# Attention and feed-forward on one core: the ones product in the projections' bank, GpSimd's additions and DMAs moved within a period, three pieces of the plan moved

## The chip, the core and the metric

The kernel runs on one NeuronCore of a Trainium2 chip. The core has five engines that run side by side, each through its own list of instructions in order: TensorE (PE in the profile; its weight loads are shown apart as PEld), VectorE (DVE), ScalarE (ACT), GpSimd (POOL) and SyncE (SP, which here only issues DMAs). [...] The metric is the device time of one execution in microseconds (us); lower is better.

## What is computed

A transformer block on `x` of shape (4, 1024, 512): attention with 16 heads of 32, then a feed-forward layer (FFN) with dequantised integer weights, each with a layer norm before and after and a residual sum.

```python
scores = jnp.einsum('bsnh,btnh->bnst', k, q) / math.sqrt(HEAD_SIZE)
scores = jnp.triu(scores) + -10000.0 * jnp.tril(ones, k=-1)
attn = jax.nn.softmax(scores, axis=2)
out = jnp.einsum('bnkq,bknh->bqnh', attn, v)
...
x = x + _layernorm(_L0_attn_ref(_layernorm(x), Wqkv, bqkv, Wo, bo))
x = x + _layernorm(_L0_ffn_ref(_layernorm(x), gate_w, gate_scale, up_w, up_scale, down_w, down_scale))
```

Each column of the attention weights is divided by the sum of its exponentials. That sum is what the ones product, the additions and the DMAs of this case make.

## The kernel before

**Steps and periods.** Attention goes by steps `(b, hb, g)`: batch `b` of 4, block `hb` of four heads (4 of them), half `g` of the 1024 queries (512 each): 32 steps. A step has 4 key tiles `c` of 128 when `g` is 0 and 8 when `g` is 1, since later keys are masked. One key tile of one step is a **period**; there are 192, after a run-in of 12 (`LEAD`). The last four tiles of a step (`c >= 4*g`) lie on the diagonal and narrow: 512, 384, 256 and 128 queries.

**A period.** Its body (line 803 on) is written out by hand and sets every engine's order. It goes through two halves `u` of two heads each. In a half, `weights` (346) has PE make scores into a PSUM tile `st`, ACT takes the exponential into the tile `pT` in SBUF (384), and on diagonal tiles GpSimd masks `pT` (386). `maxima` (259) makes the scores `sc` of a later step, and DVE takes their maximum (286, 290). `add_up` (425) adds the preceding tile's `pT` to the step's running total. One entry of the list `later` is taken. In half 0 PE also does `values` (395): the product `po` of the masked `pT` of the tile **before** with `v`. So a mask made in one period is read by PE in the next.

**The sum of exponentials.** `add_up` acts for the tile before. Whole-width tiles (`c <= 4*g`) are added by two accumulating DMAs that GpSimd issues (438), both in half 0; narrower ones by GpSimd itself (441), one pair of heads in each half. These stand on GpSimd's queue between the masks of the two halves. The last tile of a step is not added. Instead `quotients` (472), in the second period of the next step, multiplies the total and the last tile by ones (`sums`, 414): the ones product `pd`, in a bank of the pool `ps_big`. DVE adds `t2` to it (482), and reciprocals (486, DVE) and quotients `o` (489, GpSimd) follow from `later`. The last two steps (`direct`) sum on PE alone, in the bank of `ps_own`.

**PSUM banks.** `ps_big` has two buffers in turn, for `sc`, half of the `st`, transposes and most else. `ps_st` and `ps_acc` have one each. `ps_own` has one, for the first projection of a half: `projected` (238) gives that one out when `state["first"]` is set, and then takes `ps_big`.

**Sum of v.** For the masked part of the softmax, `later_v` (551) makes `vl`, a running sum of `v`, with one DVE scan over 1024 columns (556). `vl` has one buffer: the scan may write it only after GpSimd has used the old one in `sums` (337) of `shared` (339). It is called by `turn_piece` (692) for the second half of `v`.

**The plan.** Projections, norms, transposes and output projections are pieces in lists with a due time and a test when they are ready. `fill_whole` (775) takes at most one piece of `whole` in half 0 of a period; only if there was none does `fill` take a projection at that place. More projections go at the end of the period (842).

**Towards the FFN.** `store_out` (579) norms and stores an output tile; that of the last tile of a batch directly follows its projection. `ffn_stage` (625) makes the first normed rows of the FFN during the last steps: statistics (`mean_rstd`, 70: two instructions on DVE, two on GpSimd), then in the same stage the normed rows (`normalized`, 85, DVE), and in the next stage their transpose (633) and its split into two parts (635, 636). After attention, `ffn` runs the rest, bound by its matmuls (965, 998).

Of the kernel before, what the change touches and what calls it, by code (L numbers as in the profile page):

```python
# [27 lines left out]
def tile_attn_ffn_sandwich(  # L28
# [70 lines left out]
    with ExitStack() as actx:  # L99
# [221 lines left out]
        def masked_part(step):  # L321

            b, hb, g = step
            mT, vl = state["mT", step], state["vl", b, hb]
            pb = ps_big.tile([P, 512], F32, tag="big", name=f"pb_{b}_{hb}_{g}")
            nc.tensor.matmul(pb, lhsT=sel, rhs=mT, start=True, stop=True)
            t1 = e2.tile([P, 512], F32, tag="t1", name=f"t1_{b}_{hb}_{g}")
            nc.scalar.activation(t1, pb, AF.Exp, bias=masked)
            t2 = e2.tile([P, 512], F32, tag="t2", name=f"t2_{b}_{hb}_{g}")

            def counts():
                if g == G - 1:
                    nc.gpsimd.memset(t1[:, 511:512], 0.0)
                nc.gpsimd.tensor_tensor(t2, behind[:, ts(g, 512)], t1, ALU.mult)

            def sums():
                nc.gpsimd.tensor_tensor(t1, t1, vl[:, 512 * g + 1 : 512 * g + 513], ALU.mult)

            def shared():
                sums()  # L340
                count(("shared", step))

            later[:0] = (counts, shared)
            state["extra", step] = t1, t2
# [77 lines left out]
                    stop=stop,  # L422
                )

        def add_up(step, c, u):

            if c == 0 or c == 4 * step[2] + 3 or step in direct:
                return  # L430
            n = width(step, c)
            pairs = [
                [t[:, k : k + 2] for t in (state["sum", step], state["pT", step, c])]
                for k in range(0, HPB, 2)
            ]
            if c <= 4 * step[2]:
                for total, pT in pairs if u == 0 else []:
                    nc.gpsimd.dma_start(total, pT, accum_op=ALU.add)  # L438
            else:
                total, pT = pairs[u]  # L440
                nc.gpsimd.tensor_tensor(  # L441
                    total[:, :, 512 - n :], total[:, :, 512 - n :], pT[:, :, :n], ALU.add
                )

        def finish(step):
            b, hb, g = step
# [25 lines left out]
        def quotients(step):  # L472
            b, hb, g = step
            o = state["o", b, hb]
            t1, t2 = state.pop(("quotients", step))
            if step in direct:
                pd = state["pd"]
            else:
                pd = ps_big.tile([P, 512], F32, tag="big", name=f"pd_{b}_{hb}_{g}")
                sums(pd, state.pop(("sum", step)), 512, True, False)  # L480
                sums(pd, state["pT", step, 4 * g + 3], P, False, True)
            nc.vector.tensor_tensor(t2, pd, t2, ALU.add)

# [77 lines left out]
        def project_out(b, j, half):  # L561
            if half == 0:
                xo = e2.tile([P, H], F32, tag="xo", name=f"xo_{b}_{j}")
                nc.sync.dma_start(xo, x[b, j * P : (j + 1) * P, :])
                state["y"] = e2.tile([P, H], F32, tag="y", name=f"y_{b}_{j}"), xo
            y, xo = state["y"]
            py = projected(f"py_{b}_{j}_{half}")
            by_columns(
                py, [(state["o", b, c][:, ts(j, P)], wo_sb[:, c, ts(half, 256)]) for c in range(HC)]
            )  # L570
            nc.vector.tensor_tensor(y[:, ts(half, 256)], py, bo_sb[:, ts(half, 256)], ALU.add)  # L571
            if half == 0 and ("quarter", b, j) in state:
                state.pop(("quarter", b, j))()
            if half == 1:
                if ("ymv", b, j - 1) in state:
                    store_out(b, j - 1)
                state["ymv", b, j] = mean_rstd(p4, [y], f"o{b}_{j}"), y, xo

        def store_out(b, j):
            mv, y, xo = state.pop(("ymv", b, j))  # L580
            normalized(y, y, mv, 0)
            nc.gpsimd.tensor_tensor(xo, xo, y, ALU.add)
            nc.sync.dma_start(x2[b, j * P : (j + 1) * P, :], xo)
# [40 lines left out]

        def ffn_stage(i):
            if i < GT:
                row = pre["rows"][:, i, :]
                mv = mean_rstd(p4, [row], f"f{i}")
            if i > 0:
                xn = state.pop(("xn2", i - 1))  # L630
                pt = ps_big.tile([P, HC, P], F32, tag="big", name=f"xt2_{i - 1}")
                for c in range(HC):
                    nc.tensor.transpose(pt[:, c, :], xn[:, ts(c, P)], ident)
                hi, lo = (pre[k][:, :, ts(i - 1, P)] for k in ("hi", "lo"))
                nc.scalar.copy(hi, pt)
                nc.vector.tensor_tensor(lo, pt, hi, ALU.subtract)
            if i < GT:
                xn = e2.tile([P, H], F32, tag="xn", name=f"xn2_{i}")
                normalized(xn, row, mv, 0)
                state["xn2", i] = xn  # L640
            if i < 3:

                k = "gud"[i]
                nc.vector.tensor_scalar_add(pre[k], pre["raw"].pop(0), -ZERO_POINT)
                pre["raw"].append(load_raw(*((0, "d", 0), (1, "u", 1), (1, "g", 0))[i]))
            if i == 3:
                pre["raw"].reverse()
# [13 lines left out]

        FULL = 1.75
        lanes = {k: [] for k in ("qk", "v", "out")}
        whole = {k: [] for k in ("rows", "ln", "turn")}
        emitted = {}

        def put(lane, cost, due, ready, f, *args):
            lane.append((cost, due, ready, f, args))

        def count(what):  # L670
            emitted[what] = emitted.get(what, 0) + 1
# [20 lines left out]
        def turn_piece(b, hb, half):  # L692
            turn_v(b, hb, half)
            if half:
                later_v(b, hb)

        NQ = S // 256
        for b in range(B):
# [30 lines left out]
            for j in range(NJ):  # L729
                for half in range(2):  # L730
# [1 line left out]
                    put(lanes["out"], FULL, min(due, n_periods - 1 if j < 4 else n_periods + 9),  # L732
                        lambda p, t=after - 4 + WAIT if j < 4 else after + 4 + WAIT: p >= t,
                        project_out, b, j, half)
            put(lanes["out"], 0.1, due, lambda p: True, store_out, b, NJ - 1)

        def heads(of, p):
            return sorted(
# [34 lines left out]
                most -= 1  # L773

        def fill_whole(p):
            ahead = sorted(heads(whole, p), key=lambda h: h[1] != "rows")
            if ahead:
                piece(whole[ahead[0][1]])
            return bool(ahead)
# [23 lines left out]
        for p in range(-LEAD, n_periods + 1):  # L803
# [4 lines left out]
            if rest:  # L808
                rest.pop(0)()
            state["last"] = bool(before) and before[0] in direct  # L810
            for u in range(2):
                state["first"] = True
                if now and (unit or u == 0):

                    weights(*now, [u] if unit else range(2))
                if unit and now:
                    maxima(*unit, [1 - u])
                elif unit and u == 0:
                    maxima(*unit, range(2), alone=True)

                if before:
                    add_up(*before, u)
                if later:
                    later.pop(0)()
                if u == 0:
                    if p in ends:
                        quotients(ends[p])
                    if before:
                        values(*before)
                        if before[1] == 4 * before[0][2] + 3:  # L830
                            finish(before[0])

                    if not fill_whole(p) and (
                        not now or now[1] - 4 * now[0][2] > 1 or spare[0] > 1.5 * FULL
                    ):
                        fill(p, 1)
# [9 lines left out]
                    look(n)  # L846
            if p > at[B - 1, HC - 1, 0] - LEAD and not pre and not (lanes["qk"] or lanes["v"]):
                ffn_begin()
                for i in range(GT + 1):
                    put(whole["ln"], 0, n_periods, lambda q, t=p + 3 + i: q >= t, ffn_stage, i)  # L850
                put(whole["ln"], 0, n_periods, lambda q: True, check_weights)
        for k in ("rows", "ln", "turn"):
            assert not whole[k], (k, len(whole[k]))
        while later:
            later.pop(0)()
# [267 lines left out]
```

## Time and profile before

| what | us |
|---|---|
| runs | 1966.08, 1966.87, 1971.24 (median 1966.87) |
| the profiled execution | 1965.28, of which the span is 1963.3 |
| mean granted clock of TensorE | 0.987 |
| attention, about 0 to 1240 | PE idle for some 90 |
| FFN, 1240 to 1963 | PE idle for some 10 |
| one masking, 128x256 (L386), median | 0.408 |
| one addition on GpSimd (L441): 128x768, 128x512 | about 1.8, 1.3 |
| issue of one accumulating DMA (L438), median | 0.874 |
| the same DMA, issue to landing: least, median, most | 4.5, 5.9, 8.4 |
| the DVE scan (L556), median | 2.28 |

A row of the waits names the engine and line that waited, what it waited for, the total in us, how often, and the longest. A row of a timeline gives the start, the duration, the engine, line and operation, what is written and read, the shape, and in brackets the idle time before it and what ended that. A row of the windows gives the busy time of each engine within the stretch, then the granted clock of TensorE (1.00 is full speed).

### The profile page before, as it was taken

How to read it: one execution, taken by the hardware profiler on the slowest of the kernel's cores; microseconds unless marked ns; L12 is line 12 of the kernel's file. 1: busy time of each engine (PE TensorE's matmuls, PEld its weight loads, DVE VectorE, ACT ScalarE, POOL GpSimd, SP SyncE). 2: the span in 40 equal slices, each digit the busy share in tenths (PEclk: the TensorE clock that was granted, in tenths of full speed). 3: DMA queues.
4: the chain of work that ended last, by engine and by line, in shares of the span. 5: the costliest groups of instructions: out<-in, count | busy, mean ns of one | idle time of the engine just before them, and what ended most of it. 6: DMA issues, size and time to landing. Idle time of an engine off the chain costs nothing. (4 is left out here: it accounts for less than half of the span.)

```text
span 1963.3 us, 40917 instructions
## 1 busy us (share of the span) xinstructions
PE 1861.1 (95%) x17761; PEld 1105.1 (56%) x17761; DVE 1205.7 (61%) x1913; ACT 643.8 (33%) x962; POOL 708.0 (36%) x1016
## 2 busy tenths in 40 slices
PE   7899899999999999989999989999999999999997
PEld 3344444444444444444443334788888888888886
DVE  4788787886786776776676774554343444434444
ACT  2244444434424443424434323122222222222221
POOL 2255555464465464564454454101010110101011
PEclk9899999999999999999999989999999999999999
DMA  3164356344244234244134441521010101001000
GB/s 113 60 140 100 80 114 123 83 109 90 57 114 98 39 83 87 63 106 87 29 59 87 114 119 60 177 97 43 1 43 1 44 6 38 33 12 44 0 22 24
DMA packets 65627, 137.48 MB, mean 70 GB/s; under 512 B 6304, under 2 KB 20640, under 8 KB 65440
## 3 DMA queue, kind: packets, MB, share of 16 engines
q0 software_dynamic: 17280, 62.92, 17.4%
q1 hardware_dynamic: 41008, 67.40, 10.4%
q10 hardware_dynamic: 7152, 4.46, 0.8%
q8 instruction: 141, 2.31, 0.5%
q14 instruction: 46, 0.38, 0.1%
HBM read 55.07 MB, written 16.78 MB: 37 GB/s over the span
## 5 line engine op out<-in xcount | busy, mean ns | idle before, releaser
L384 ACT ACTIVATE pT<-st 128x1024 f32<-128x1024 f32 (+3 forms) x384 | 310.2, 811 | 363.7 <-PE st L367 307.0
L290 DVE TENSOR_REDUCE nm<-sc 128x2 f32<-128x1024 f32 (+3 forms) x384 | 366.7, 956 | 101.7 <-PE st L367 82.4
L250 PE MATMUL pq<-xnT,w 128*32 128x256 f32 x6144 | 379.2, 388 | 3.5 <-ACT xnT L520 2.7
L278 PE MATMUL sc<-in,in 32*128 32x512 f32 (+3 forms) x1536 | 349.1, 540 | 18.8 <-DVE nm L290 18.5
L367 PE MATMUL st<-in,in 32*128 32x512 f32 (+3 forms) x1536 | 307.0, 489 | 0.0
L250 PEld LDWEIGHTS pq<-xnT,w 128*32 128x32 f32 x6144 | 191.0, 111 | 201.7 <-issue 89.3
L975 DVE SCALAR_TENSOR_TENSOR h<-pu,pre_us,s 128x512 f32<-128x512 f32 x128 | 96.1, 751 | 311.4 <-PE pu L965 310.7
L386 POOL TENSOR_SCALAR_AFFINE_SELECT pT<-pT 128x256 f32<-128x256 f32 x256 | 120.9, 480 | 294.1 <-ACT pT L384 290.7
L998 PE MATMUL acc<-d,h 128*128 128x512 f32 x896 | 224.8, 393 | 0.2 <-DVE h L985 0.2
L286 DVE TENSOR_TENSOR sc<-sc,bound 128x256 f32<-128x256 f32 x256 | 109.1, 426 | 149.5 <-PE sc L278 93.6
L406 PE MATMUL po<-pT,vt 128*32 128x512 f32 (+3 forms) x1536 | 181.7, 499 | 17.9 <-POOL pT L386 17.8
L441 POOL TENSOR_TENSOR pT<-pT,pT 128x768 f32<-128x768 f32 (+1 forms) x120 | 186.2, 1552 | 16.6 <-DMA pT<-pT 16.6
L973 ACT ACTIVATE s<-pg,pre_gs 128x512 f32<-128x512 f32 x128 | 88.1, 688 | 297.5 <-PE pg L965 297.5
L998 PEld LDWEIGHTS acc<-d,h 128*128 128x128 f32 x896 | 166.1, 188 | 34.2 <-DVE h L985 0.5
L79 POOL TENSOR_SCALAR rs_y<-mv_y 128x1 f32<-128x1 f32 x32 | 8.7, 272 | 448.4 <-DVE mv_y L77 448.4
L984 ACT CAST h<-h 128x512 fp32r<-128x512 f32 x128 | 79.5, 621 | 249.7 <-DVE h L975 249.7
L438 POOL DMA_DIRECT2D pT<-pT x120 | 106.3, 939 | 123.4 <-PE pm L314 61.6
L359 PE MATMUL st<-mT,ones_bf 3*128 3x512 bf16 (+3 forms) x768 | 125.6, 333 | 19.9 <-ACT pT L384 19.7
L985 DVE TENSOR_TENSOR h<-h,h 128x512 fp32r<-128x512 f32 x128 | 88.6, 692 | 87.9 <-ACT h L984 87.9
L278 PEld LDWEIGHTS sc<-in,in 32*128 32x128 f32 x1536 | 115.5, 185 | 39.1 <-issue 21.9
L367 PEld LDWEIGHTS st<-in,in 32*128 32x128 f32 x1536 | 134.9, 191 | 0.6
L250 PE MATMUL py<-wo_sb,o 128*32 128x256 f32 x2048 | 124.6, 387 | 5.5 <-DVE y L571 3.4
(136 smaller groups left out, 2581.1 us busy)
## 6 DMA issues: line engine op xcount, KB each, us to landing
pT<-pT POOLq DMA_DIRECT2D x120, 512.0 KB, 5.9
xr<-in_x SPq DMA_DIRECT2D x32, 256.0 KB, 3.2
xo<-in_x SPq DMA_DIRECT2D x32, 256.0 KB, 2.8
x<-xo SPq DMA_DIRECT2D x32, 256.0 KB, 2.0
out<-y SPq DMA_DIRECT2D x32, 256.0 KB, 2.0
look<-in_gate_wt SPq DMA_DIRECT2D x16, 256.0 KB, 3.1
look<-in_up_wt SPq DMA_DIRECT2D x16, 256.0 KB, 2.9
look<-in_down_wt SPq DMA_DIRECT2D x16, 256.0 KB, 3.5
```

The lines of the kernel that those rows point to most:

```text
L250: nc.tensor.matmul(out[k * D : (k + 1) * D, :], lhsT=lhsT[:, k * D : (k + 1) * D], rhs=rhs, start=(c == 0), stop=(c == len(pairs) - 1),)
L278: nc.tensor.matmul(sc[:, h % 2, :n], lhsT=qT[h * D : (h + 1) * D, ts(j, P)], rhs=kT[h * D : (h + 1) * D, 512 * k : 512 * k + n], start=Tru ...
L286: nc.vector.tensor_tensor(sc[:, :, n - P : n], sc[:, :, n - P : n], bound.unsqueeze(1).to_broadcast((P, 2, P)), ALU.min,)
L290: nc.vector.tensor_reduce(nm[:, k, jj, 2 * u : 2 * u + 2], sc[:, :, :n], AX.X, ALU.max, negate=True)
L359: nc.tensor.matmul(st[h // 2][:, h % 2, :n], lhsT=ones_bf[h * D : h * D + 3, :], rhs=mT[h * D : h * D + 3, 512 - n :], start=True, stop=False,
L367: nc.tensor.matmul(st[h // 2][:, h % 2, :n], lhsT=kT[h * D : (h + 1) * D, ts(c, P)], rhs=qT[h * D : (h + 1) * D, q0 : q0 + n], start=False ...
L384: nc.scalar.activation(pT[:, :, :n], st[u][:, :, :n], AF.Exp)
L386: nc.gpsimd.affine_select(out=pT[:, :, :P], in_=pT[:, :, :P], compare_op=ALU.is_ge, fill=0.0, base=0, pattern=[[0, 2], [1, P]], channel_mu ...
L406: nc.tensor.matmul(state["po"][h * D : (h + 1) * D, 512 - n :], lhsT=v[:, c, h * D : (h + 1) * D], rhs=pT[:, h, :n], start=(c == 0), stop= ...
L438: nc.gpsimd.dma_start(total, pT, accum_op=ALU.add)
L441: nc.gpsimd.tensor_tensor(total[:, :, 512 - n :], total[:, :, 512 - n :], pT[:, :, :n], ALU.add)
L998: nc.tensor.matmul(acc[t0][t], lhsT=part[:, ts(t, P)], rhs=dw[i * P // IB][:, i % (IB // P), :], start=(i == 0 and k == 0), stop=(i == IC ...
```

## The change

Nothing is added to or taken from what the engines execute: the number of instructions of each kind on each engine is the same. What moves:

1. `add_up` is called once at the start of a period for its DMAs (`wide=True`), ahead of both maskings, and once in half 1 for GpSimd's own additions, behind both maskings, both pairs of heads in a row.
2. `pd` is made in `ps_own`, and the first projection behind it in that half goes to `ps_big`.
3. `later_v` becomes a piece of its own (`scan`), ready two periods after `shared` of the step before, ahead of all but `rows`. It takes a place of `fill_whole`. In 12 of the 16 head blocks it now stands in the period of the second diagonal tile (`c = 4*g + 1`), and other pieces move back by a place.
4. `ffn_stage` norms rows one stage after their statistics and transposes them a stage later: six stages instead of five.
5. `store_out` of the last tile of a batch may be taken only in a later period than its projection.

```diff
-        def add_up(step, c, u):
-            if c == 0 or c == 4 * step[2] + 3 or step in direct:
+        def add_up(step, c, wide):
+            if c == 0 or c == 4 * step[2] + 3 or step in direct or wide != (c <= 4 * step[2]):
                 return
             n = width(step, c)
-            pairs = [
-                [t[:, k : k + 2] for t in (state["sum", step], state["pT", step, c])]
-                for k in range(0, HPB, 2)
-            ]
-            if c <= 4 * step[2]:
-                for total, pT in pairs if u == 0 else []:
+            for k in range(0, HPB, 2):
+                total, pT = (t[:, k : k + 2] for t in (state["sum", step], state["pT", step, c]))
+                if wide:
                     nc.gpsimd.dma_start(total, pT, accum_op=ALU.add)
-            else:
-                total, pT = pairs[u]
-                nc.gpsimd.tensor_tensor(
...
+                else:
+                    nc.gpsimd.tensor_tensor(
...
-                pd = ps_big.tile([P, 512], F32, tag="big", name=f"pd_{b}_{hb}_{g}")
+                state["first"] = False
+                pd = ps_own.tile([P, 512], F32, tag="own", name=f"pd_{b}_{hb}_{g}")
...
             if half == 1:
                 if ("ymv", b, j - 1) in state:
                     store_out(b, j - 1)
+                state["rows at", b, j] = state["p"]
...
             if i < GT:
-                row = pre["rows"][:, i, :]
-                mv = mean_rstd(p4, [row], f"f{i}")
-            if i > 0:
-                xn = state.pop(("xn2", i - 1))
+                state["mv2", i] = mean_rstd(p4, [pre["rows"][:, i, :]], f"f{i}")
+            if i > 1:
+                xn = state.pop(("xn2", i - 2))
...
-            if i < GT:
-                xn = e2.tile([P, H], F32, tag="xn", name=f"xn2_{i}")
-                normalized(xn, row, mv, 0)
+            if 0 < i <= GT:
+                xn = e2.tile([P, H], F32, tag="xn", name=f"xn2_{i - 1}")
+                normalized(xn, pre["rows"][:, i - 1, :], state.pop(("mv2", i - 1)), 0)
...
             if half:
-                later_v(b, hb)
+                free = emitted.get(("shared", steps[steps.index((b, hb, 0)) - 1]), -99) + 2
+                put(whole["scan"], 0, at[b, hb, 0] - 1, lambda p: p >= free, later_v, b, hb)
...
-            put(lanes["out"], 0.1, due, lambda p: True, store_out, b, NJ - 1)
+            put(lanes["out"], 0.1, due + 1,
+                lambda p, b=b: state.get(("rows at", b, NJ - 1), p) < p, store_out, b, NJ - 1)
...
-            ahead = sorted(heads(whole, p), key=lambda h: h[1] != "rows")
+            ahead = sorted(heads(whole, p), key=lambda h: h[1] not in ("rows", "scan"))
...
+            if before:
+                add_up(*before, wide=True)
             for u in range(2):
...
-                if before:
-                    add_up(*before, u)
+                if before and u == 1:
+                    add_up(*before, wide=False)
                 if later:
                     later.pop(0)()
```

`emitted["shared", step]` now holds the period in which `shared` was issued instead of a count.

More of the change, by code (lines that the diff above doesn't have):

```diff
@@ L340, in shared @@
                 sums()
-                count(("shared", step))
+                emitted["shared", step] = state["p"]
             later[:0] = (counts, shared)
@@ L423, in sums @@
                 )
-        def add_up(step, c, u):
-            if c == 0 or c == 4 * step[2] + 3 or step in direct:
+        def add_up(step, c, wide):
+            if c == 0 or c == 4 * step[2] + 3 or step in direct or wide != (c <= 4 * step[2]):
                 return
             n = width(step, c)
-            pairs = [
-                [t[:, k : k + 2] for t in (state["sum", step], state["pT", step, c])]
-                for k in range(0, HPB, 2)
-            ]
-            if c <= 4 * step[2]:
-                for total, pT in pairs if u == 0 else []:
-                    nc.gpsimd.dma_start(total, pT, accum_op=ALU.add)
-            else:
-                total, pT = pairs[u]
-                nc.gpsimd.tensor_tensor(
-                    total[:, :, 512 - n :], total[:, :, 512 - n :], pT[:, :, :n], ALU.add
-                )
+            for k in range(0, HPB, 2):
+                total, pT = (t[:, k : k + 2] for t in (state["sum", step], state["pT", step, c]))
+                if wide:
+                    nc.gpsimd.dma_start(total, pT, accum_op=ALU.add)
+                else:
+                    nc.gpsimd.tensor_tensor(
+                        total[:, :, 512 - n :], total[:, :, 512 - n :], pT[:, :, :n], ALU.add
+                    )
         def finish(step):
@@ L626, in ffn_stage @@
             if i < GT:
-                row = pre["rows"][:, i, :]
-                mv = mean_rstd(p4, [row], f"f{i}")
-            if i > 0:
-                xn = state.pop(("xn2", i - 1))
-                pt = ps_big.tile([P, HC, P], F32, tag="big", name=f"xt2_{i - 1}")
+                state["mv2", i] = mean_rstd(p4, [pre["rows"][:, i, :]], f"f{i}")
+            if i > 1:
+                xn = state.pop(("xn2", i - 2))
+                pt = ps_big.tile([P, HC, P], F32, tag="big", name=f"xt2_{i - 2}")
                 for c in range(HC):
                     nc.tensor.transpose(pt[:, c, :], xn[:, ts(c, P)], ident)
-                hi, lo = (pre[k][:, :, ts(i - 1, P)] for k in ("hi", "lo"))
+                hi, lo = (pre[k][:, :, ts(i - 2, P)] for k in ("hi", "lo"))
                 nc.scalar.copy(hi, pt)
                 nc.vector.tensor_tensor(lo, pt, hi, ALU.subtract)
-            if i < GT:
-                xn = e2.tile([P, H], F32, tag="xn", name=f"xn2_{i}")
-                normalized(xn, row, mv, 0)
-                state["xn2", i] = xn
+            if 0 < i <= GT:
+                xn = e2.tile([P, H], F32, tag="xn", name=f"xn2_{i - 1}")
+                normalized(xn, pre["rows"][:, i - 1, :], state.pop(("mv2", i - 1)), 0)
+                state["xn2", i - 1] = xn
             if i < 3:
@@ L663, in tile_attn_ffn_sandwich @@
         lanes = {k: [] for k in ("qk", "v", "out")}
-        whole = {k: [] for k in ("rows", "ln", "turn")}
+        whole = {k: [] for k in ("rows", "ln", "turn", "scan")}
         emitted = {}
@@ L810, in tile_attn_ffn_sandwich @@
             state["last"] = bool(before) and before[0] in direct
+            state["p"] = p
+            if before:
+                add_up(*before, wide=True)
             for u in range(2):
@@ L848, in tile_attn_ffn_sandwich @@
                 ffn_begin()
-                for i in range(GT + 1):
+                for i in range(GT + 2):
                     put(whole["ln"], 0, n_periods, lambda q, t=p + 3 + i: q >= t, ffn_stage, i)
                 put(whole["ln"], 0, n_periods, lambda q: True, check_weights)
-        for k in ("rows", "ln", "turn"):
+        for k in ("rows", "ln", "turn", "scan"):
             assert not whole[k], (k, len(whole[k]))
```

## The prediction

> **What bounds the kernel now.** I read the page's first part, then PE's own waits, then timelines around the longest of them, and last the busy times in the stretch where attention gives way to the FFN. The chain of waits is of little use: it goes back only to 1245.9 us, into the FFN, whose matmuls follow each other without a pause and which the change leaves alone.
>
> ```profile
> PE 1861.1 (95%) x17761; PEld 1105.1 (56%) x17761; DVE 1205.7 (61%) x1913; ACT 643.8 (33%) x962; POOL 708.0 (36%) x1016
> ```
>
> PE is the bound, and its 102.2 us of idle time (1963.3 - 1861.1) are what a reordering can win. In windows of 40 us it is busy for 1189.0 of the first 1280, so 91 of them lie there, some 20 before 80 us, which the change hardly touches. PE's waits:
>
> ```profile
> PE st L359 <- ACT pT L384: 19.7, 39, 1.1
> PE sc L278 <- DVE nm L290: 18.5, 11, 3.5
> PE po L406 <- POOL pT L386: 17.8, 21, 1.8
> ...
> PE pd L417 <- PE st L367: 4.9, 7, 1.0
> ...
> PE pd L417 <- DVE nm L290: 3.3, 4, 1.1
> ...
> PE pd L417 <- issue: 2.4, 2, 1.2
> ```
>
> Three rows are aimed at: `po` waits for masks, `pd` for its bank, and part of `sc`, whose bank a late DVE holds. The waits for ACT stay.
>
> **The change part by part.** *Maskings against DMAs and additions.* GpSimd and PE in the period of a second diagonal tile:
>
> ```profile
> 128.23 0.41 POOL L386 TENSOR_SCALAR_AFFINE_SELECT pT<-pT 128x256 f32<-128x256 f32 x1 [0.40 <-ACT pT L384]
> 128.72 0.88 POOL L438 DMA_DIRECT2D pT<-pT  x1
> 132.01 0.85 POOL L438 DMA_DIRECT2D pT<-pT  x1 [2.41 <-DMA pT<-pT]
> ...
> 133.78 0.77 POOL L386 TENSOR_SCALAR_AFFINE_SELECT pT<-pT 128x256 f32<-128x256 f32 x2
> ```
>
> ```profile
> 131.88 0.84 PE L406 MATMUL po<-pT,vt 128*32 128x384 f32 x4
> 134.23 0.84 PE L406 MATMUL po<-pT,vt 128*32 128x384 f32 x4 [1.51 <-POOL pT L386]
> ```
>
> The second DMA waits for the landing of the previous tile's DMA, and the mask of half 1, whose exponential ended at 130.3, stands behind it. Eight steps show this at 384 queries; the gaps add to 8.65 us. After the change the previous tile's DMAs go ahead of that period's mask too, about 2.9 us earlier (122.89 against a period that starts near 120). The accumulating DMAs land some 4 us apart, nearly back to back, so I count on 1.5 us, not 2.9: landing near 130.0, issue until 130.9, masks at 131.3 and 131.7, just before PE asks at 131.9. Queued behind the DMA's wait is now the mask of half 0 as well; it has 3 us of slack. In 12 periods of this kind the scan arrives too. In its old period it stretched a mask beside it to 2.17 us instead of 0.41. I charge 0.2 us each, some 2 in all. Value -6.6; bounds -8.7 (all gone) and +3 (the scan holds both masks until 1 us past PE's wish, twelve times: 12 - 8.7).
>
> At 256 queries the gaps add to 1.3; one of 0.75 is a mask behind an addition that waited for a DMA, now out of its way: -0.8, bounds -1.3 and 0. At 128 queries they add to 8.0. There the additions of two pairs, 2 x 1.82, now stand together behind the mask before and in front of the next ones. With T the end of the last exponential at 256 queries and g = 0, GpSimd needs 0.41 + 3.64 + 1.28 (L334) + 0.41 until the first mask of the last tile (T + 5.74), then 1.10 (L337) and 0.41 (T + 7.25). In one step of the trace T is 950.8 and PE asks at 957.3 for the first half, 0.4 later for the second: wait 0.35 where it was 0.56. Steps with 1.2 to 1.8 us gain or lose some 0.3. With g = 1 nothing else stands between, and T + 4.9 is in time. Value -0.5, bounds -3 and +10.
>
> *The ones product.* Its waits without the two behind DVE's own additions add to 10.8. In `ps_own` it finds the bank emptied by ACT in the period before. But the next user of `ps_big` soon waits for the same DVE reduction: in the step at 283 us the product could start 1.2 us sooner, while the following `st` tile would get its bank only 0.6 sooner. I take half, -5.4; bounds -10.8 and 0. What is late next is DVE (L482), which must empty `ps_own` before the end-of-period projection; 1 us of other PE work covers it, without which each of 30 products would cost up to that.
>
> *Last store of a batch.*
>
> ```profile
> 877.00 0.55 DVE L86 TENSOR_SCALAR y<-y,mv_o 128x512 f32<-128x512 f32 x1 [1.41 <-POOL mv_o L80]
> ```
>
> DVE stands still, the maximum behind it keeps a bank, PE idles for 2.54 and then runs at half clock for 3.4 us (up to 1.7 lost). The store two periods later finds its statistics done: -3, bounds -4.2 and 0.
>
> *Scan and FFN norm*, the stretch from 1120 to 1195:
>
> ```profile
> 1124.43 0.86 POOL L438 DMA_DIRECT2D pT<-pT  x1 [3.56 <-DMA pT<-pT]
> 1124.99 1.42 POOL L337 TENSOR_TENSOR t<-t,vl 128x512 f32<-128x512 f32 x1
> ```
>
> ```profile
> 1126.44 2.29 DVE L556 TENSOR_TENSOR_SCAN vl<-in,zero 128x1024 f32<-128x1024 f32 x1 [5.98 <-POOL t L337]
> ```
>
> ```profile
> 1125.00:1130.00 5.00, 1.35 (x8) 0.50 (x7) 3.56 (x3) 1.11 (x2) 3.92 (x4) 0.81 0.57 107
> 1130.00:1135.00 5.00, 5.00 (x36) 1.89 (x40) 4.93 (x9) 0.00 (x0) 3.40 (x6) 0.51 0.14 52
> ...
> 1140.00:1145.00 5.00, 4.58 (x26) 1.83 (x26) 4.75 (x11) 0.59 (x1) 3.44 (x6) 0.67 0.77 239
> ...
> 1155.00:1160.00 5.00, 2.15 (x18) 1.48 (x22) 4.86 (x12) 0.87 (x2) 2.66 (x5) 0.88 0.44 153
> ```
>
> GpSimd waits for a DMA, DVE's scan for GpSimd, PE for the maximum behind the scan (3.51). Four norms of FFN rows wait for GpSimd too (1.71, 1.53, 0.43, 1.69). From 1120 to 1160 PE is idle for 10.5 of 40 us and the clock dips. But DVE is busy for 29.7 of those 40, so it becomes the bound when its waits go: at best 10 are won. It won't run without a pause: -6. Near 1186 the last store of batch 2 (1.42 on DVE) makes part of a PE gap of 2.31 before another dip: -2. Together -8; bounds -17 (13.7 idle from 1120 to 1195, and some of the half speed) and +2 (the scan now in the midst of DVE's fullest periods).
>
> *The clock.* It falls to half in six stretches between 100 and 1240 us, 27.3 us together, behind gaps of 2.54, 1.06, 3.51, 2.48, 2.15 with 1.32, and 2.31 us. [...]
>
> *Sum.* -6.6 - 0.8 - 0.5 - 5.4 - 3 - 8 = -24.3. A PE that comes sooner meets exponentials and masks that were just in time (many end 0.1 to 0.4 us before they are read): I give back a fifth, 4.9. So 1965.3 - 19.4 = 1945.9. That is against the profiled execution's own time, 1.6 under the median of the runs; I say 1946.
>
> **Rivals.** *The waits move on.* Removing each bank or mask wait only uncovers the next: DVE in the last stretch, ACT elsewhere (19.7 us in 39 waits). For it: DVE's 29.7 of 40. Against it: the two long stalls of DVE are idle time of every engine. Then about 1 from the store and 3 from the scan remain: 1961.
> *Slower: the row of additions.* Two additions stand in front of the next masks, where one stood. If PE asks for the last tile early, each of 30 steps waits. The 24.3 of gains are eaten at 0.8 us a step; at 1.1 it is 33, and the time 1974. For it: the first step, where PE asks at T + 4.7. Against it: elsewhere PE asks at T + 5.0 to 8.5, against 4.9 (g = 1) and 7.25 (g = 0).
> *More goes.* All waits for masks from 256 and 384 queries, all of `pd` and the store, and 14 in the last stretch, with dips: 8.7 + 1.3 + 10.8 + 4.2 + 14 = 39, less 4: 1930.
> *The bank is not free.* If a projection still sits in `ps_own`, `pd` gains nothing: 1965.3 - 18.9 + 3.8 (a fifth) = 1950.
>
> **How the numbers follow.** Forecast 0.58, with 1936 to 1958 of its own; waits move on 0.15; slower 0.11; more 0.10; bank 0.06. The range 1930 to 1963 leaves out the slow case and the ends. Three tenths of a per cent, 5.9 us, is about what a measurement here tells from no change. Faster by more than that (under 1961): 0.56 of the forecast's 0.58, 0.10, 0.06 and 0.06 of the first rival, together 0.78; slower 0.11; the rest 0.11.
>
> **What would show it.** Right: no wait of `po` at 384 queries; the DVE scan never waiting for L337; `pd` waits under 5; PE idle under 5 between the place of 1120 and 1160; no dip near 879. Wrong: `po` waits at 128 queries over 15 us in all, masks behind a scan in the second diagonal tile's period, or `st` and `sc` waits grown by what the others lost.

## The result and the profile after

The changed kernel takes 1952.55 us (median of four runs, 1948.84 to 1954.0) where the kernel before takes 1967.62 beside it (1966.08 to 1971.24). The ratio is 0.9916, with a 95% interval of 0.9902 to 0.9931: 14 to 19 us less, against the 21 that were forecast. The profiled execution has a span of 1951.2 us, 12.1 below the span before, at a granted clock of 0.985.

PE's line in the first part of the page of the changed kernel, and then its waits:

```profile
PE 1862.9 (95%) x17761; PEld 1103.4 (57%) x17761; DVE 1224.9 (63%) x1913; ACT 643.6 (33%) x962; POOL 713.0 (37%) x1016
```

```profile
PE st L359 <- ACT pT L384: 21.9, 42, 1.1
PE sc L278 <- DVE nm L290: 17.7, 16, 3.9
PE po L406 <- POOL pT L386: 11.0, 12, 2.9
PE py L250 <- DVE y L567: 6.9, 4, 3.0
...
PE sc L278 <- DVE y L567: 2.4, 2, 1.2
...
PE pd L417 <- DVE y L567: 1.2, 2, 0.8
PE pd L417 <- DVE t L478: 0.9, 1, 0.9
```

The waits aimed at did shrink: `po` from 17.8 to 11.0, `pd` from 13.0 in all to 2.0. What should catch the eye is the other half. PE's idle time fell by 13.9 us (102.2 to 88.3), but PE's busy time grew by 1.8 and DVE's by 19.2, with the same instructions. Waits for DVE's reading of output projections (`py` and `sc` on L567) are new or doubled.

Where the 12 us come from is seen by cutting the span at the same instruction in both traces. From the end of the second step's last exponential to that of the first step of the last batch, both kernels take the same time. The windows of just this stretch, before and then after:

```profile
140.70:956.10 815.40, 774.60 (x9935) 350.40 (x9928) 611.88 (x934) 325.69 (x479) 443.69 (x612) 1.00 0.40 87
```

```profile
141.40:956.90 815.50, 781.46 (x9943) 350.13 (x9936) 630.01 (x937) 326.12 (x480) 449.28 (x614) 0.99 0.40 87
```

PE idles 6.8 us less here and is busy 6.9 us longer. In this stretch TensorE was at half speed (a granted clock of 0.50) for 3.4 us before and for 20.5 after. By an estimate, half of these 17.1 us more, that alone can make PE's work up to 8.5 us longer. DVE is busy 18 us longer. So two thirds of attention gained nothing, and the whole 12 us came after 956 us. There PE's idle time up to its last matmul fell by 7 (28.6 to 21.6), and half speed up to 1240 us from 23.9 to 10.2 us.

### The profile page after: what moved, and what is told of

Its sections match the earlier page's. It is cut to its first block, busy times and chain, and to the rows that moved or that the text cites. A ratio compares the mean times of both kernels' runs of the same rounds, so it can differ in the third digit from the quotient of the medians.

```text
span 1951.2 us, 40980 instructions
## 1 busy us (share of the span) xinstructions
PE 1862.9 (95%) x17761; PEld 1103.4 (57%) x17761; DVE 1224.9 (63%) x1913; ACT 643.6 (33%) x962; POOL 713.0 (37%) x1016
## 3 DMA queue, kind: packets, MB, share of 16 engines
q1 hardware_dynamic: 41008, 67.40, 10.2%
q8 instruction: 141, 2.31, 0.5%
## 4 chain that ended last, share of the span: by engine, by line
PE 83%; DVE 8%; POOL 3%; ACT 2%; DMA 2%; issue 1%; POOLq 0%; DVEq 0%
PE pq L250 18%; PE pg L966 12%; PE pu L966 12%; PE acc L999 12%; PE sc L278 9%; PE po L406 6%; PE st L359 4%; PE st L367 4%; PE py L250 3%; PE pd L417 2%; DVE nm L290 2%; DMA pT<-pT 2%; ACT pT L384 2%; PE pv L544 1%; POOL xo L579 1%
## 5 line engine op out<-in xcount | busy, mean ns | idle before, releaser
L278 PE MATMUL sc<-in,in 32*128 32x512 f32 (+3 forms) x1536 | 348.4, 540 | 20.1 <-DVE nm L290 17.7
L386 POOL TENSOR_SCALAR_AFFINE_SELECT pT<-pT 128x256 f32<-128x256 f32 x256 | 131.1, 535 | 261.7 <-ACT pT L384 261.5
L406 PE MATMUL po<-pT,vt 128*32 128x512 f32 (+3 forms) x1536 | 172.6, 497 | 11.1 <-POOL pT L386 11.0
```

What stands on the lines that cost most here:

```text
L278: nc.tensor.matmul(sc[:, h % 2, :n], lhsT=qT[h * D : (h + 1) * D, ts(j, P)], rhs=kT[h * D : (h + 1) * D, 512 * k : 512 * k + n], start=Tru ...
L386: nc.gpsimd.affine_select(out=pT[:, :, :P], in_=pT[:, :, :P], compare_op=ALU.is_ge, fill=0.0, base=0, pattern=[[0, 2], [1, P]], channel_mu ...
L406: nc.tensor.matmul(state["po"][h * D : (h + 1) * D, 512 - n :], lhsT=v[:, c, h * D : (h + 1) * D], rhs=pT[:, h, :n], start=(c == 0), stop= ...
```

## The experiments

All of them are the kernel before or after with parts of the change put in or out. Each kernel was run 4 to 12 times. Runs of one kernel beside each other differ by up to 13.5 us (the kernel before, 20 runs), and span and granted clock move against each other: 1975.6 at 0.981 and 1969.9 at 0.984 in one kernel. So beside the ratio the table gives span times clock, the median over the runs less the same for the kernel before beside them. It is an estimate of what the time would be with no stretch at half speed. Single runs of one kernel still scatter by 2.4 to 9.9 us in it, so a difference of two medians under some 3 us can't be told from none. (For the whole change it is against the one profiled execution of before.) What a change does to the clock is left out of it; the ratio has that too. "Chain" is the time from L301 to L306 on DVE, five small operations on 128x16 at the end of each step, summed over 32 steps.

| kernel | ratio to before (95%) | span x clock, us | `po` waits for masks, us | chain, us |
|---|---|---|---|---|
| before | 1 | 0 | 17.8 | 73.4 |
| b_add: part 1 | 1.0039 (1.0024 to 1.0053) | +1.5 | 6.0 | 98.9 |
| b_ones: part 2 | 0.9959 (0.9946 to 0.9971) | -8.0 | 19.2 | 74.4 |
| b_scan: part 3 | 1.0011 (1.0002 to 1.0020) | -1.4 | 18.4 | 76.4 |
| b_rows: parts 4, 5 | 0.9964 (0.9951 to 0.9977) | -5.2 | 22.7 | 74.6 |
| b_store: part 5 | 0.9956 (0.9942 to 0.9971) | -4.5 | 18.3 | 73.8 |
| b_add_ones: 1, 2 | 0.9924 (0.9911 to 0.9938) | -15.2 | 6.1 | 98.8 |
| b_ones_rows: 2, 4, 5 | 0.9893 (0.9878 to 0.9908) | -11.3 | 22.9 | 74.8 |
| a_noscan: 1, 2, 4, 5 | 0.9876 (0.9860 to 0.9892) | -18.4 | 9.6 | 96.2 |
| a_noadd: 2, 3, 4, 5 | 0.9882 (0.9867 to 0.9897) | -13.0 | 25.5 | 75.6 |
| the whole change | 0.9916 (0.9902 to 0.9931) | -15.9 | 11.0 | 97.1 |
| c_add: 2, 4, 5, additions of 1 | 0.9980 (0.9966 to 0.9994) | -3.7 | 19.4 | 96.4 |
| c_dma: 2, 4, 5, DMAs of 1 | 0.9835 (0.9814 to 0.9857) | -26.7 | 14.5 | 69.4 |
| a_dma: 2 to 5, DMAs of 1 | 0.9814 (0.9795 to 0.9832) | -26.9 | 11.2, and 3.6 more (below) | 71.9 |

**Part 1 alone** (b_add): the kernel before with

```diff
+            if before:
+                add_up(*before, wide=True)
             for u in range(2):
...
-                if before:
-                    add_up(*before, u)
+                if before and u == 1:
+                    add_up(*before, wide=False)
```

> The kernel before with the first part alone: the DMAs of a period go ahead of both maskings, GpSimd's own additions behind both. Theory of the prediction (a removed wait is time): PE's waits for masks (17.8 us before, 11.0 after the whole change) fall to 8 to 11, the waits at 384 queries before 1100 us to under 1, and the time falls by 6 (to about 1961). Rival, waits move on: the masks are early but PE waits as long for something else; idle time of PE falls by less than 2 and the time stays within 2 of before. Rival, the clock takes it: PE's idle time falls by 5 to 8, but stretches at half clock are added between 102 and 956 us, and the time falls by less than half of the idle time.

It is 7.7 us slower by the ratio. The waits for masks went as far as hoped, those at 384 queries to 0.01 us. But the ones product, which waited 3.3 us for DVE's maxima, now waits 20.0:

```profile
PE pd L417 <- DVE nm L290: 20.0, 15, 2.2
...
PE po L406 <- POOL pT L386: 6.0, 7, 1.7
```

The first reading, that PE merely comes sooner to a bank still held, was not enough. DVE itself is late. Its chain and GpSimd's additions at the end of one step, before and after (the start, the duration, then the operation):

```profile
142.33 0.17 DVE L301 TENSOR_TENSOR nm<-nm,least 128x16 f32<-128x16 f32 x1
...
142.54 0.20 DVE L303 CAST wide<-nm 128x16 bf16<-128x16 f32 x1
...
142.78 0.18 DVE L304 TENSOR_TENSOR nm<-nm,wide 128x16 f32<-128x16 f32 x1
143.00 0.21 DVE L305 CAST wide<-nm 128x16 bf16<-128x16 f32 x1
...
143.24 0.35 DVE L306 TENSOR_TENSOR wide<-nm,wide 128x16 bf16<-128x16 f32 x1
...
143.49 1.27 POOL L441 TENSOR_TENSOR pT<-pT,pT 128x512 f32<-128x512 f32 x1
```

```profile
144.51 2.49 POOL L436 TENSOR_TENSOR pT<-pT,pT 128x512 f32<-128x512 f32 x2
144.63 1.19 DVE L304 TENSOR_TENSOR nm<-nm,wide 128x16 f32<-128x16 f32 x1
...
145.85 1.21 DVE L305 CAST wide<-nm 128x16 bf16<-128x16 f32 x1
...
147.10 0.35 DVE L306 TENSOR_TENSOR wide<-nm,wide 128x16 bf16<-128x16 f32 x1
```

Operations of 0.18 and 0.21 us take 1.19 and 1.21: each starts just behind the start of an addition and ends as that ends. Over all 32 chains 30 of the 160 operations take over 0.7 us before and 56 after, most often one in a chain before (16 chains) and two after (17); 21 and 47 of these end with an addition of GpSimd, the others with another of its operations on two tiles (L337 or L334, lines of `masked_part`). The same in b_add pushes back the maximum that empties the bank of the product, 5 us on:

```profile
144.39 1.20 DVE L305 CAST wide<-nm 128x16 bf16<-128x16 f32 x1
...
145.63 0.34 DVE L306 TENSOR_TENSOR wide<-nm,wide 128x16 bf16<-128x16 f32 x1
...
149.78 1.22 DVE L290 TENSOR_REDUCE nm<-sc 128x2 f32<-128x1024 f32 x1
...
151.29 1.29 PE L417 MATMUL pd<-pT,ones 128*32 128x512 f32 x14 [1.94 <-DVE nm L290]
```

Before, that maximum started at 147.94 and the product at 149.36 with no gap.

**Part 2 alone** (b_ones):

```diff
-                pd = ps_big.tile([P, 512], F32, tag="big", name=f"pd_{b}_{hb}_{g}")
+                state["first"] = False
+                pd = ps_own.tile([P, 512], F32, tag="own", name=f"pd_{b}_{hb}_{g}")
```

> The kernel before with the second part alone: the ones product in the projections' bank. Theory of the prediction: the waits of the ones product (13.1 us in all before) fall under 3 and the time falls by 4 (half of the waits without DVE's own additions, less a fifth). Rival, waits move on: the projection behind the ones product now takes a bank of the other pool, and PE waits for DVE's reading of output projections instead (3.4 us in 6 waits before, 9 and more after): time within 2 of before. Rival, the clock takes it: idle time falls by 5 or more and comes back as half clock.

It gives 8.0 us by span and clock, and 9.4 by the medians: more than the theory's 4. The waits of the ones product fell from 13.0 to 5.2, not under 3. Those of `py` for output projections stayed at 3.3, so the rival that waits move on falls. Half speed between 102 and 1240 us was 23.9 us (27.3 before), so the clock did not take it either.

**Part 3 alone** (b_scan):

```diff
-                later_v(b, hb)
+                free = emitted.get(("shared", steps[steps.index((b, hb, 0)) - 1]), -99) + 2
+                put(whole["scan"], 0, at[b, hb, 0] - 1, lambda p: p >= free, later_v, b, hb)
```

> The kernel before with the third part alone: the running sum of v as a piece of its own. Theory of the prediction: the 5.98 us wait of the scan for GpSimd goes, the long PE gap near 1126 us with it, time less by 4 to 5. Rival, the scan collides: where it lands in the period of a step's last tile, with the chain of small reductions (lines 300 to 306 of DVE), DVE reads output projections late, PE waits 2 to 3 us near 575 and 862 us, and the time is within 2 of before.

The theory is right on the gap and wrong on the time. The scan no longer waits for GpSimd, and the gap of 3.51 near 1126 us is gone. But the gap before the next product of `sc`, 2.48 before the change (near 1138), is now 4.81, because DVE waits 4.60 for the statistics of an FFN row (1.71 before):

```profile
1142.44 0.62 DVE L86 TENSOR_SCALAR xn<-pre_rows,mv_f 128x512 f32<-128x512 f32 x1 [4.60 <-POOL mv_f L80]
...
1145.67 1.65 PE L278 MATMUL sc<-in,in 32*128 32x384 f32 x4 [4.81 <-DVE nm L290]
```

So the wait moved on, to what part 4 is meant to move. Gaps of 1.15 and 1.40 near 575 and 1.38 at 870 stand at the ends of batches; they are smaller than the rival's 2 to 3.

**Parts 4 and 5 alone** (b_rows):

```diff
-                xn = e2.tile([P, H], F32, tag="xn", name=f"xn2_{i}")
-                normalized(xn, row, mv, 0)
...
+                xn = e2.tile([P, H], F32, tag="xn", name=f"xn2_{i - 1}")
+                normalized(xn, pre["rows"][:, i - 1, :], state.pop(("mv2", i - 1)), 0)
...
-            put(lanes["out"], 0.1, due, lambda p: True, store_out, b, NJ - 1)
+            put(lanes["out"], 0.1, due + 1,
+                lambda p, b=b: state.get(("rows at", b, NJ - 1), p) < p, store_out, b, NJ - 1)
```

> The kernel before with the fourth and fifth part: rows of the FFN normed a stage after their statistics, the last output tile of a batch stored in a later period. Theory of the prediction: the PE gap of 2.54 us near 876 and its stretch at half clock go (3), four waits of DVE for statistics of FFN rows (5.4 us) go, together 5 less time. Rival, GpSimd and DVE are full there: DVE's waits go, but PE's idle time from 1100 to 1200 stays within 2 of the 14 before, and the time falls by 2 to 3 from the store alone.

The size is the theory's by span and clock (5.2), and 8.5 by the medians. PE's idle time from 1100 to 1200 us falls from 14.8 to 10.0, so the rival that it stays within 2 falls. Part 5 by itself (the last lines of this diff):

> The kernel before with the store of a batch's last output tile alone moved to a later period. Theory of the prediction: the PE gap of 2.54 near 876 goes and nothing takes its place but what stood before: 3 less. Since this and the FFN rows together gave 8.5 (5.2 with the clock left out), the rows would then be worth 2 to 5. Rival: the store is worth nothing by itself, because a wait for a mask of about 2.5 us takes the place of the gap (as it stands near 857 in the kernel with both), and all of it came from the FFN rows: within 2 of before.

It gives 4.5 (8.8 by the medians), so the FFN rows alone are worth 0.7, within what can be told. The rival named its trace rightly, though not the time: a wait for a mask of 2.47 at 860 us takes the place of the gap at 876. By the gaps over 0.3 us PE waits only 1.7 less between 850 and 900 us. The gap of 2.31 before the product near 1186 is down to 0.33, and its half speed is gone.

**Pairs and the change less one part.** b_add_ones and b_ones_rows put parts together; a_noadd and a_noscan undo one, with the diffs above.

> The kernel before with the first and second part. Theory, bank first: the first part turns from a loss of 8 into a gain of 5 to 7 beside the second, so the two together give 9.4 + 6 = 15 (1950 to 1953); waits of the ones product under 4, waits for masks under 9. Rival, they add: -9.4 + 8.3 = -1, 1965 to 1967. Rival, worth nothing: as the second part alone, 1957 to 1959.

> The changed kernel with the first part undone (DMAs and additions where they stood). Theory, bank first: alone the first part only moved 12 us of waits from masks to the ones product, whose bank a late DVE holds; where that product has a bank of its own the early masks are time, and undoing them costs 5 to 7: 1958 to 1960, with waits for masks back at 17 or more. Rival, worth nothing: the gains of the parts simply add and the first part is worth nothing with any neighbour: 1951 to 1954. Rival, the clock: undoing it takes stretches at half clock away too, and the kernel is faster than the changed one, 1946 to 1950.

> The changed kernel with the third part undone (the running sum of v directly behind the transpose). Theory of the prediction: the 5.98 us wait of the scan for GpSimd is back, with a PE gap of 3 or more between 1110 and 1140, and the time is 3 to 5 above the changed kernel: 1955 to 1958. Rival, from the third part alone (1970 against 1967): the scan's new places cost PE 1 to 3 us each at the end of a batch, and without them the time is 1946 to 1950, with the gap of 3.04 near 862 gone.

> The kernel before with the second, fourth and fifth part, without the first and third. If the gains add: -9.4 - 8.5 = -18, 1949. Theory, bank first: the same, and the first part would still take 5 from it. Rival, both free the same late DVE near 1120 to 1160 us: less than the sum, 1953 to 1956.

Beside part 2, part 1 turns from +1.5 into -7.2 (-15.2 against -8.0), as "bank first" says. b_ones_rows is close to the sum. But without part 1 the whole change is not 5 to 7 us slower; it is faster (0.9882 against 0.9916), and without part 3 too (0.9876): 1947.67 and 1946.58, each within its rival's 1946 to 1950. For a_noadd that rival is the clock: it rises from 0.985 to 0.988, while by span and clock part 1 is worth 2.9 there, which is within the scatter. In a_noscan the scan waits 6.3 for GpSimd again and the gap of 3.59 before `sc` is back, as the theory says, and the kernel is faster all the same.

**Part 1 in halves.** The row of additions was the suspect, so the two halves were parted, both without part 3. c_dma keeps the DMAs ahead and puts one addition back into each half:

```diff
-            for k in range(0, HPB, 2):
+            for k in range(0, HPB, 2) if wide else [2 * u]:
...
-                if before and u == 1:
-                    add_up(*before, wide=False)
+                if before:
+                    add_up(*before, False, u)
```

c_add has no early DMAs:

```diff
-            if before:
-                add_up(*before, wide=True)
...
-                if before and u == 1:
-                    add_up(*before, wide=False)
+                if before:
+                    add_up(*before, wide=u == 0)
```

> The changed kernel without the third part, and of the first part only the DMAs: they go ahead of both maskings, but GpSimd's additions stand one in each half, as before. Theory, the row of additions holds DVE: the chain of small DVE operations at the end of a step (lines 301 to 306), 73 to 76 us in 32 steps where additions stand apart and 96 to 99 where two stand in a row, is back at 73 to 77; waits for masks at 384 queries before 1100 us under 1; faster than with both halves of the part (ratio 0.9876) and than without it (0.9893): 0.983 to 0.986, about 1938 to 1943. Rival, the additions' place is half the gain: waits for masks stay over 15, and the ratio is 0.987 to 0.990.

> The same, with the other half alone: additions in a row behind both maskings, DMAs between the maskings as before. Theory, the row of additions holds DVE: the chain takes 96 to 99 us, the waits at 384 queries stay (8 us), and the time is no better than without the first part: ratio 0.988 to 0.992. Rival, the additions' place is the gain: waits for masks under 12 and a ratio under 0.987.

Both came as the theory said, and c_add further: 0.9980 is on the slow side of its 0.988 to 0.992. Against b_ones_rows the DMAs alone give 15.4 us by span and clock, and the additions cost 7.6. Together they give 7.1 (a_noscan), so within the scatter the halves add. By the ratios it is 11 and 17 us, since the clock takes part.

Three pairs of kernels differ in the additions' place alone: b_ones_rows and c_add, c_dma and a_noscan, and a_dma (below) and the changed kernel. In each the row makes PE wait longer for what DVE reads late: `sc` for maxima 13.8 to 17.2, 14.3 to 18.1 and 14.0 to 17.7 us, and `sc` for output projections from 0 to 1.8, 1.8 and 2.4. Waits for masks do not grow (22.9 to 19.4, 14.5 to 9.6, and 11.2 to 11.0). Half speed from 85 to 1240 us goes from 23.9 to 41.0, 23.9 to 37.5 and 20.5 to 34.1 in the profiled executions, and the median clock over the runs falls too (0.989 to 0.985, 0.988 to 0.9865, 0.990 to 0.985).

This accounts for the two thirds of attention that gained nothing. From the end of the second step to that of the first step of the last batch, the profiled executions take 815.4 us before, 807.6 with parts 2, 4 and 5 (b_ones_rows), 795.6 with the DMAs moved too (c_dma), 810.4 with the additions in a row (a_noscan) and 815.5 with part 3 (the changed kernel).

**The changed kernel with its additions put back** (a_dma), the edit of c_dma in the whole change:

> The changed kernel in full, but with GpSimd's additions one in each half, as before; the DMAs stay ahead of the maskings. Theory, the row of additions is what the change lost: the chain of small DVE operations is back under 78 us (97 in the changed kernel), the ratio comes to 0.983 to 0.987, 8 to 16 us faster than the changed kernel, level with the same kernel without the third part (0.9835). Rival, the third part collides by itself: the waits of PE for output projections near 560 and 860 us stay (6.9 us in the changed kernel) and the ratio is 0.987 to 0.991. Rival, the additions were not it: 0.990 to 0.993, as the changed kernel.

1930.75 us, 36 below the kernel before and some 20 below the changed one (0.0102 of 1967), the fastest of all and beyond the theory's range. Its page:

```profile
PE 1845.9 (96%) x17761; PEld 1098.1 (57%) x17761; DVE 1204.6 (62%) x1913; ACT 643.1 (33%) x962; POOL 714.0 (37%) x1016
```

DVE is back from 1224.9 to 1204.6 with the same instructions, the chain is 71.9, and the clock was 0.990 or 0.991 in all five runs. The first rival is right that waits near 560 and 845 stay (5.8 us of `py` waits) and wrong in the price: part 3 costs nothing that can be told here (0.9814 against 0.9835, with overlapping intervals). Beside the row of additions it does cost (0.9916 against 0.9876). The longest wait left in attention is 3.63 us at 1114, before `po`, where the masks are late; the trace puts it down to a small operation of GpSimd between them (L551), so it is not among the 11.2.

## Why the prediction was right, and where it was not

The forecast (faster, 1946) had the direction, and its range held the time. Its sum was near by luck: two errors in it nearly cancelled.

**Maskings at 384 queries: mis-sized.** The gaps went as forecast (8.65 to 2.88, all of that one wait at 1135). The step counted the gap alone. A late second half also splits the eight matmuls of `po`. Where the prediction showed two groups of 0.84 us each, the changed kernel has:

```profile
134.43 0.85 PE L406 MATMUL po<-pT,vt 128*32 128x384 f32 x8
```

At 384 queries and full clock eight in a row take 0.91 us on average (24 steps before), and split 1.68 beside the gap (8 steps); at 128 queries 0.43 against 0.83. So the 8.65 of gaps stood for 8 x 0.77 = 6.2 more, 14.8 together. In c_dma, against b_ones_rows, these gaps fall by 8.5 and the splits at 384 from 8 to 1, which makes 8.5 + 5.4 = 13.9; 15.4 was measured.

**The row of additions: wrong in its reason.** The step looked for masks that come late to PE at 128 queries and said -0.5, with a bound of +10. These waits fell (8.0 to 5.8). The cost was elsewhere, 7.6 us by span and clock and more with the clock: the row stands beside DVE's chain, 23.7 us longer over 32 steps, and the maxima behind it hold banks, as the three pairs show. The rival "slower: the row of additions" was the right suspect with the wrong victim. It wins outright only where the ones product shares the bank of the maxima (b_add). The prediction had a mask beside the scan at 2.17 us instead of 0.41 and did not ask what else of DVE's meets an addition.

**The ones product: too cautious.** "I take half, -5.4" measured -8.0. The waits fell by 7.8 in b_ones and by 11.0 in the changed kernel, and the gaps that the next tile was to keep did not appear in b_ones (`st` waits 19.0 for exponentials, 19.7 before).

**Last store: right in size.** -3 here and -2 near 1186 measured -4.5 together. But at the first place a wait for a mask took most of what the gap gave (2.47 against 2.54); that the sum holds all the same is in part luck.

**Scan and FFN norm: half right.** Each alone is worth 1.4 and 0.7, against the -6. The gaps near 1126 and 1138 need one part each: part 3 takes away the first and lengthens the second (b_scan), part 4 takes away the second and leaves 3.50 of the first (b_rows). With both parts neither is left. From the end of the 29th step to that of the last (1095.1 to 1218.3 before) it takes 123.1 us before, 119.3 with the store alone and 115.6 in the changed kernel. Three pairs differ in part 3 alone, all with parts 2, 4 and 5. With it this stretch is shorter: 119.5 to 115.0 (b_ones_rows, a_noadd), 121.0 to 114.2 (c_dma, a_dma), 118.6 to 115.6 (a_noscan, the changed kernel). But from the second step to the first of the last batch the same pairs take 4.6, 3.8 and 5.1 us longer with it, where the sum had charged some 2 for the scan's new places. PE's idle time from 1120 to 1160 is 8.7, not under 5. DVE waits for GpSimd's statistics no longer there, and PE waits for its mask:

```profile
1130.90 2.44 POOL L485 TENSOR_TENSOR o<-t,t 128x128 f32<-128x128 f32 x1
1133.31 1.28 POOL L579 TENSOR_TENSOR xo<-xo,y 128x512 f32<-128x512 f32 x1
...
1135.37 0.93 POOL L434 DMA_DIRECT2D pT<-pT  x1
1136.80 0.87 POOL L434 DMA_DIRECT2D pT<-pT  x1 [0.49 <-DMA pT<-pT]
1137.36 0.93 POOL L386 TENSOR_SCALAR_AFFINE_SELECT pT<-pT 128x256 f32<-128x256 f32 x1
```

The mask stands behind a product that takes 2.44 us beside the scan (1130.81 to 1133.09), a residual sum, the statistics and both DMAs; PE waits 2.88 us for it. That is the rival "the waits move on", in one place, and one of the signs of being wrong: a mask behind a scan in the second diagonal tile's period. The DMAs ahead put the masks of both halves behind their landing; here, with GpSimd late already, that is part of the 2.88.

**The fifth given back** is not borne out by the parts: by span and clock the four alone sum to -13.1, and together they measured -15.9.

**The clock: wrong sign.** The prediction had half speed go at 878.9 and in the last stretch, and named none to come; 27.3 us between 102 and 1240 became 30.7. The one at 878.9 did go, but one at 864.6 came. There the scan now stands ahead of the chain, and PE waits 3.04 us for DVE to empty an output projection:

```profile
858.57 2.28 DVE L552 TENSOR_TENSOR_SCAN vl<-in,zero 128x1024 f32<-128x1024 f32 x1
...
861.66 0.65 DVE L300 TENSOR_TENSOR nm<-nm 128x16 f32<-128x16 f32 x1
862.35 1.18 DVE L301 TENSOR_TENSOR nm<-nm,least 128x16 f32<-128x16 f32 x1
...
864.36 0.42 DVE L567 TENSOR_TENSOR y<-py,bo_sb 128x256 f32<-128x256 f32 x1
```

Those at 444.8 and 738.3 follow gaps of 0.88 and 0.94 before `sc`, which waits for the maximum behind a chain of 3.3 and 3.4 us (2.5 before). Neither gap is in a_dma, where the chain takes 2.5 again. Since half speed grew in all three pairs, the row of additions has a share in it; how large that is beside the luck of the last section stays open.

## What to carry to other kernels

Price a wait in the middle of a group of matmuls at its gap plus what the group loses by being split; here a gap of 1.08 us on average cost 0.77 more by the split. Before GpSimd's work is put in a row, look which small DVE operations run beside it: here 47 of 160 took over 0.7 us and ended with an addition, where 21 had before. When a change has several parts, run each half of each part, and compare span times clock beside the times: here one half gave 15 us and the other took 8 of them back.

## What the hardware showed

**DVE held by GpSimd.** Two operations of DVE's chain that took 0.18 and 0.21 us in the kernel before took 1.19 and 1.21 beside additions. Of the 160 operations of the 32 chains, 47 take over 0.7 us and end with an addition in the changed kernel, 21 in the one before; each ends 0.03 to 0.09 us after it. In the three pairs that differ in the additions' place alone the row makes the chains 21.6 to 26.8 us longer (74.8 to 96.4, 69.4 to 96.2, 71.9 to 97.1). Why the two end together was not shown.

**Half speed came on a grid.** In each of the fourteen traces all stretches at half clock start at multiples of 3.4133 us from each other, to within 0.01 of a step, and before 1240 us they last one to three steps. In the kernel before the first and the last start, at 39.23 and 1957.53 us, are 562 steps apart, in the changed kernel 558 (38.58 and 1943.22). In both, steps with few matmuls were followed by one at half speed, as behind the 9 and the 14 here. Two pairs of windows, one of before and one of after (the busy times of PE, its weight loads, DVE, ACT and GpSimd, then the granted clock):

```profile
875.46:878.88 3.42, 0.88 (x9) 0.47 (x10) 1.97 (x5) 1.26 (x2) 2.67 (x5) 1.00 0.20 77
878.88:882.29 3.41, 3.41 (x28) 1.46 (x32) 1.71 (x3) 0.00 (x0) 3.41 (x6) 0.50 0.20 77
```

```profile
441.40:444.81 3.41, 2.38 (x14) 0.78 (x17) 3.31 (x7) 1.61 (x3) 0.81 (x2) 0.99 0.00 0
444.81:448.23 3.42, 3.42 (x32) 1.31 (x32) 2.56 (x5) 0.00 (x0) 1.42 (x3) 0.51 0.27 60
```

With the windows set 0.6 us earlier, 14 windows of these two traces between 85 and 1240 us have 14 matmul starts or fewer, and each is followed by half speed; five more stretches follow fuller ones (16 to 36 starts). In b_add shift and count fit worse (9 of 13, and 7 from fuller ones), and in the twelve other traces together 65 of 93 such windows are followed by half speed, so the measure is not settled, and what brings half speed about was not shown. In the second pair PE was busy 2.38 of 3.41 us before half speed, and its longest gap there is 0.88.

The grid does not start with the program: its first mark lies 1.68 us into the span in the kernel before and 1.03 in the changed one. So the same instructions meet it differently. The kernels before, b_store and b_rows have the same work up to the end of the first step, and reach it at 93.7, 95.8 and 91.4 us, with 17.1, 20.5 and 10.2 us at half speed by the end of the second. By an estimate from the step and its clock of 0.50, a gap may so cost its own length in one execution, and half of 3.41 us more in another.
